# Graph attention: partial sums of k and v kept in one PSUM bank, and queries of two tiles by seven half-width products

## The chip, the cores and the metric

The kernel runs on one core of a Trainium2 chip. The metric is the device time of one execution in microseconds (us), lower is better, as the median of several runs. TensorE (PE in the profile) multiplies matrices into PSUM, which has eight banks of 128 partitions by 512 f32 values; VectorE (DVE) and ScalarE (ACT) read PSUM and do the elementwise work; GpSimd (POOL) issues the gathers; SyncE (SP) issues plain transfers.

## The reference

There are 16 graphs of 1024 nodes and 512 features, 8 heads of 64, and an adjacency matrix shared by all, in which nodes of low number have many neighbours and most have few. All inputs are f32.

```python
q = (x @ Wq + bq).reshape(b, n, H, HD)
k = (x @ Wk + bk).reshape(b, n, H, HD)
v = (x @ Wv + bv).reshape(b, n, H, HD)
scores = jnp.einsum('bqhd,bkhd->bhqk', q, k) / jnp.sqrt(jnp.float32(HD))
scores = scores + (1.0 - adj)[None, None, :, :] * -1000000000.0
attn = jax.nn.softmax(scores, axis=-1)
out = jnp.einsum('bhqk,bkhd->bqhd', attn, v).reshape(b, n, d) @ Wo + bo
...
x = _layernorm(x + out, axis=-1)
```

## The kernel before

The kernel finds the neighbours of each node at run time, sorts the nodes by their number of neighbours, and gathers `k` and `v` of a neighbour row by row, so that softmax runs only over edges. In each batch (a graph) the nodes lie in eight tiles of 128. One **block** is one neighbour of each of the 128 nodes of a tile; there are 530 blocks, 32 to 34 a batch.

**The work on a block** is spread over the steps of one large loop (its counter is `n`; it starts at -39 and ends after the last block). `gather` starts the transfer of the `k` and `v` rows into a tile `kvg`; `products` multiplies `k` by the query on VectorE (`qk`), `scores` sums by head (`s`), `exponentials` runs on ScalarE, and `weigh` multiplies `v` by the weights, either on ScalarE in eight activations of 64 columns or on VectorE in one instruction: `by_act` chooses. `add_own` adds up on VectorE; blocks of the few nodes with many neighbours go through a product on TensorE (`add_up`, bank `sum`). `normalise` divides, `turn` transposes the result (`poT`), and `finish` and `complete` multiply by `Wo` (`po`, through `product`) and do the residual and the layer norm.

**The fronts** make `q`, `k` and `v` of coming batches. `transpose_x` transposes a tile of `x` (`pxT`), `combine` makes four sums of halves of two tiles (`s1` to `s4`, each 128x256) and `pair(b, j)` lists the products of tiles 2j and 2j+1 as units. A query tile takes four products of 128x512 columns (`product`, line 799) and one VectorE instruction (line 830). `k` and `v` of the two tiles together take seven products of two halves each (`unit`, line 956), in the manner of Strassen and Winograd: the weights are combined once into `T1` to `T4`, and the products are added up in five banks: `x` (twice), `z` (twice), `p6`, `p7` and `p4`. ScalarE copies the first sum to `e` and the first `k` from bank `x` (lines 969, 835), and VectorE makes `w`, `g`, the second `k` and both `v` (lines 972, 975, 979, 984, 988). `squares` gives norms that a later test uses.

**The order** is written out by hand while the program is built. Each step places a fixed set of instructions and then takes units from a list (`finishing` before `fronts`) as long as its allowance of TensorE time (`credit`, fed by `share`) lasts; the costs of units are the constants `PRODUCT`, `SUM`, `TRANSPOSE` and `BIAS` in microseconds. A unit has a `ready` condition; if the first unit in the list is not ready, the step takes none. `later(k, fn)` puts an instruction k steps on, `later_last` at the end of such a step. Each engine then runs its instructions in that order, and waits for what it needs. PSUM is divided into four banks for `fill` (`pxT`, `poT`, `pq`, `po`, `p6`, `p7`, `p4` and small ones), two for `sum`, one for `x`, one for `z`. When the fronts have ended, tiles put aside in DRAM (`SPILL`) are finished, with the output bias added by a bf16 product (`bo_3` in three pieces, line 1090).

Of the kernel before, what the change touches and what calls it, by code (L numbers as in the profile page):

```python
# [10 lines left out]
F32 = mybir.dt.float32  # L11
# [39 lines left out]
ROWS = 3  # L51
# [18 lines left out]
LEAD_SHARE = 3.3  # L70
START_SHARE = 2.0
LAST_SHARE = 3.4
BIAS = 0.22

# [104 lines left out]
def kernel(  # L179
# [75 lines left out]
    with ExitStack() as main:  # L255
# [6 lines left out]
        def fill_psum(name):  # L262
            return psum.tile([P, HALF], F32, tag="fill", name=name, bufs=4)
# [19 lines left out]
        bo_3 = one.tile([P, D], BF16, name="bo_3")  # L283
        three = one.tile([P, 1], BF16, name="three")
# [4 lines left out]
        B12 = [None]  # L289

# [66 lines left out]
        def loads():  # L357
# [3 lines left out]
            nc.vector.tensor_scalar(bq_bc, bq_bc, scale, None, op0=OP.mult)  # L361
# [27 lines left out]
            yield  # L389
            broadcast(bo_bc, bo)  # L390
# [25 lines left out]
        def bias_norms():  # L416
# [10 lines left out]
            nc.vector.tensor_tensor(bk_bc, bq_bc, bq_bc, op=OP.mult)  # L427
            nc.vector.tensor_reduce(n8, bk_bc.rearrange("p (h d) -> p h d", d=HD), axis=AX.X, op=OP.add)
            nc.vector.tensor_reduce(bq_norm, n8, axis=AX.X, op=OP.max)

        def bias_pieces():

            r = work.tile([P, D], F32, tag="y", name="bo_rest", bufs=Y_BUFS)
            nc.vector.tensor_copy(bo_3, bo_bc)
            nc.vector.tensor_tensor(r, bo_bc, bo_3, op=OP.subtract)
            yield
            nc.vector.tensor_copy(bo_3[32:33, :], r[32:33, :])
            nc.vector.tensor_copy(bo_3[64:65, :], r[64:65, :])
            nc.vector.tensor_tensor(r[64:65, :], r[64:65, :], bo_3[64:65, :], op=OP.subtract)
            nc.vector.tensor_copy(bo_3[64:65, :], r[64:65, :])  # L440
            yield
            st = small.tile([P, 1], F32, name="two", bufs=1)
            nc.vector.tensor_tensor(st, ident[:, 0:1], ident[:, 32:33], op=OP.add)
            nc.vector.tensor_tensor(three, st, ident[:, 64:65], op=OP.add)

# [15 lines left out]
        def ranks():  # L461
# [55 lines left out]
            nc.vector.tensor_scalar(lone, ranked[:, 0, 1:2], 0.0, None, op0=OP.is_le)  # L517
# [24 lines left out]
        def more_ranks():  # L542
# [44 lines left out]
            for h in range(HEADS):  # L587
                sq = work.tile([P, D], F32, tag="ysq", name=f"sq_wq_{h}", bufs=1)[:, 0:NPAIR * HD].rearrange("p (c d) -> p c d", c=NPAIR)
# [48 lines left out]
        def edges(t):  # L637
# [63 lines left out]
            for i0 in range(0, nb, step):  # L701
# [8 lines left out]
                m = work.tile([P, D], F32, tag="qk", name=f"em_{t}_{i0}", bufs=2)[:, 0:n * J].rearrange("p (n j) -> p n j", n=n)  # L710
# [26 lines left out]
        BOTH = {}  # L737
        X, XT, SX, KV, VSUM, NRM, Y, OT, PS = {}, {}, {}, {}, {}, {}, {}, {}, {}
# [13 lines left out]
        def transpose_x(b, t):  # L752
            def pe():
# [5 lines left out]
                def out():  # L759
# [3 lines left out]
                    if t == 0 and b >= PAIRED_FROM:  # L763
# [6 lines left out]
                        sq = work.tile([P, D], F32, tag="ysq", name=f"sq_x_{b}", bufs=1)  # L770
# [9 lines left out]
                def combine():  # L780
                    s = [work.tile([P, HD2], F32, tag=f"s{i}", name=f"s{i}_{b}_{t}", bufs=1 + i // 4) for i in (1, 2, 3, 4)]
# [9 lines left out]
            return [(TRANSPOSE, pe, lambda: (b, t) in X)]  # L791

        def product(name, lhs, w, out):

            def unit(c):
                if c == 0:
                    PS[name] = fill_psum(name)
# [6 lines left out]
            return [(PRODUCT, lambda c=c: unit(c), None) for c in range(NPAIR)]  # L804
# [11 lines left out]
        def pair(b, j):  # L816
# [8 lines left out]
            def out_q(i, p):  # L825

                assert gathered[0] >= start[max(0, b - ROWS + 1)]
                tag, bufs = ("q", 2) if b or j else ("y", Y_BUFS)
                q = work.tile([P, D], F32, tag=tag, name=f"q_{b}_{tt[i]}", bufs=bufs)
                nc.vector.scalar_tensor_tensor(q, p, scale, bq_bc, op0=OP.mult, op1=OP.add)  # L830
# [34 lines left out]
            def mean_pe():  # L865
# [3 lines left out]
                def out():  # L869
                    m = work.tile([1, D], F32, tag="q", name=f"mean_{b}", bufs=2)  # L870
# [8 lines left out]
            def lone_product():  # L879
# [24 lines left out]

                return [(4 * BIAS, pe, None)]

            def lhs(i):
                return lambda c: XT[b, tt[i]][:, ts(c, P)]

            q0, q1 = (  # L910
                product(f"pq_{b}_{tt[i]}", lhs(i), W["q"], lambda p, i=i: out_q(i, p)) if b == 0 or tt[i] != ONE_KEY else []
                for i in range(2)
            )
            if j == 0 and b >= PAIRED_FROM:
                q0 = []
                if merged(b):
                    q0 = product(f"pq_{b}_0", lambda c: BOTH[b // 2][:, 1, c, :], W["q"], lambda p: out_q(0, p))
                    q0 += lone_product()
# [29 lines left out]
            def unit(bank, left, right, first, after, need):  # L948
                def pe():
                    if first:  # L950
                        R[bank] = fill_psum(f"p{bank}_{b}_{j}") if bank[0] == "p" else psum.tile(
                            [P, HALF], F32, tag=bank, name=f"{bank}_{b}_{j}", bufs=1
                        )
                    l = left()
                    for c in range(2):
# [6 lines left out]
                return [(2 * PRODUCT, pe, lambda: (need is None or need in R) and (b, j) in SX and bool(combined))]  # L962

            def temp(name):
                R[name] = work.tile([P, D], F32, tag=name, name=f"{name}_{b}_{j}", bufs=1)
                return R[name]

            def out_e():
                nc.scalar.copy(temp("e"), R["x"])  # L969

            def out_w():
                nc.vector.tensor_tensor(temp("w"), R["p6"], R["e"], op=OP.add)

            def out_g():
                nc.vector.tensor_tensor(temp("g"), R["p7"], R["w"], op=OP.add)

            def out_k1():
                kv = KV[b, tt[1]]
                nc.vector.tensor_tensor(kv[:, 0:D], R["p4"], R["g"], op=OP.add)  # L979
                send(1)  # L980
                later_last(1, lambda: norm(b, tt[1], kv[:, 0:D]))

            def out_v1():
# [674 lines left out]
```

## Time and profile before

| | us |
|---|---|
| median of 3 runs | 1856.82 |
| lowest, highest | 1855.36, 1866.84 |
| span of the profiled execution, first to last instruction | 1840.4 |
| PE, DVE, ACT, POOL busy in it | 1798.2, 1693.7, 1563.2, 1215.3 |

The runs are timed from outside the program, and the profile's span runs from the first to the last instruction of the program; the profiled execution's own time is given by its span alone. In the profile's rows a line such as L956 is a line of the kernel; out<-in names tiles without their numbers; after a count come the busy time in us, the mean length of one instruction in ns, and the idle time of the engine just before, with what ended it. Each f32 product appears as two matmul instructions. Their lengths overlap, since matmuls are pipelined and their ends are modelled. PEld is the loading of weights, and beside a stretch the granted clock of TensorE and the share of the DMA engines are given.

### The profile page before, as it was taken

Reading aid. Unit: us, or ns where it says so; the run is one execution under the profiler, and the core shown is the slowest. Engines: PE = TensorE matmul, PEld = TensorE weight load, DVE = VectorE, ACT = ScalarE, POOL = GpSimd, SP = SyncE. Lnnn points to the kernel's source line nnn. Section 1 sums busy time; section 2 is a strip of 40 time slices with the busy share of each in tenths; the row PEclk is TensorE's granted clock in tenths of the full one; section 3 lists DMA queues with packets and bytes.
Section 4 is the critical chain, followed back from the end, with each engine's and each line's share of the span. In section 5 each row is a group of like instructions: output and inputs, shape, how many; then the busy total and the mean of one; then the engine's idle time right before and its main releaser. Section 6 shows DMA issues by size and latency. Waiting matters only on the chain.

```text
span 1840.4 us, 25352 instructions
## 1 busy us (share of the span) xinstructions
PE 1798.2 (98%) x5140; PEld 876.2 (48%) x5140; DVE 1693.7 (92%) x3473; ACT 1563.2 (85%) x6183; POOL 1215.3 (66%) x1142
## 2 busy tenths in 40 slices
PE   7999999999999999999999999999999999999997
PEld 3444454554444454444444445444544444444443
DVE  6889889999989999999999999999999999997986
ACT  3637869989889898999889988989799999987886
POOL 1367766766565776767757666677666767665786
PEclk9999999999999999999999999999999999999998
DMA  7358787989889899999988998999989999889995
GB/s 287 106 190 253 256 325 237 346 301 327 308 280 314 295 336 319 344 316 308 347 316 310 346 335 276 343 321 322 339 315 325 314 355 326 306 324 325 338 319 191
DMA packets 198791, 558.54 MB, mean 303 GB/s; under 512 B 33450, under 2 KB 33470, under 8 KB 198626
## 3 DMA queue, kind: packets, MB, share of 16 engines
q0 software_dynamic: 112640, 370.50, 59.3%
q1 hardware_dynamic: 82910, 180.52, 26.2%
q10 hardware_dynamic: 3076, 5.82, 0.9%
q14 instruction: 122, 1.00, 0.2%
q8 instruction: 43, 0.70, 0.2%
HBM read 420.30 MB, written 157.45 MB: 314 GB/s over the span
## 4 chain that ended last, share of the span: by engine, by line
PE 69%; DVE 10%; ACT 9%; DMA 4%; issue 3%; POOL 1%; SPq 0%; POOLq 0%; DVEq 0%; ACTq 0%
PE po L799 17%; PE pq L799 15%; PE pp L956 12%; PE z L956 9%; PE x L956 9%; ACT pv L1341 5%; DVE qk L1313 2%; PE poT L1401 2%; PE pxT L757 2%; PE sum L1367 2%; DVE s L1317 2%; PE sum L1366 2%; DVE pv L1357 1%; ACT sq_k L809 1%; DMA kvg<-kv_pair,place_row 1%
## 5 line engine op out<-in xcount | busy, mean ns | idle before, releaser
L1341 ACT ACTIVATE pv<-kvg,pv 128x64 f32<-128x64 f32 x3600 | 907.5, 341 | 0.0
L1292 POOL DMA_INDIRECT kvg<-kv_pair,place_row x462 | 526.7, 1140 | 307.4 <-ACT pv L1341 99.6
L799 PE MATMUL pq<-wq,xT 128*128 128x512 f32 x792 | 367.8, 596 | 0.0
L1317 DVE TENSOR_REDUCE s<-qk 128x8 f32<-128x512 f32 x530 | 360.7, 681 | 6.8
L799 PE MATMUL po<-wo,oT 128*128 128x512 f32 x792 | 359.3, 594 | 0.7 <-ACT oT L1405 0.7
L1313 DVE TENSOR_TENSOR qk<-qt,kvg 128x512 f32<-128x512 f32 x434 | 297.2, 685 | 1.1 <-DMA kvg<-kv_rows,key_row 0.6
L956 PE MATMUL x<-b,xT 128*128 128x512 f32 x504 | 237.3, 593 | 0.5 <-ACT e L969 0.4
L956 PE MATMUL pp<-t,s 128*128 128x512 f32 x504 | 237.0, 593 | 0.0
L1357 DVE TENSOR_TENSOR pv<-pv,pv 128x520 f32<-128x520 f32 x329 | 228.3, 694 | 4.3 <-ACT pv L1341 4.2
L799 PEld LDWEIGHTS po<-wo,oT 128*128 128x128 f32 x792 | 149.1, 191 | 170.0 <-issue 160.2
L799 PEld LDWEIGHTS pq<-wq,xT 128*128 128x128 f32 x792 | 148.4, 192 | 161.9 <-issue 149.9
L1010 POOL DMA_INDIRECT x<-in_x_dram,asked_row x120 | 133.0, 1108 | 77.8 <-issue 21.3
L1148 POOL DMA_INDIRECT out_dram<-y,asked_row x129 | 146.9, 1139 | 39.1 <-issue 21.2
L1328 ACT ACTIVATE pv<-s,absent 128x8 f32<-128x8 f32 x434 | 127.0, 294 | 44.0 <-DVE s L1317 40.8
L809 ACT ACTIVATE sq_k<-kv 128x128 bf16<-128x128 f32 x512 | 150.8, 301 | 6.4 <-DVE kv L979 3.4
L956 PEld LDWEIGHTS pp<-t,s 128*128 128x128 f32 x504 | 94.7, 191 | 108.1 <-issue 99.4
L956 PEld LDWEIGHTS x<-b,xT 128*128 128x128 f32 x504 | 94.2, 191 | 107.4 <-issue 99.0
L956 PE MATMUL z<-b,s 128*128 128x512 f32 x252 | 119.2, 596 | 7.0 <-DVE kv L984 7.0
L1246 POOL DMA_INDIRECT qg<-q_rows,query_row x96 | 104.4, 1088 | 28.4 <-issue 26.9
L956 PE MATMUL z<-t,s 128*128 128x512 f32 x252 | 118.6, 593 | 0.0
L956 PE MATMUL pp<-t,xT 128*128 128x512 f32 x252 | 118.5, 593 | 0.0
L1134 ACT ACTIVATE y<-y,stats 128x512 f32<-128x512 f32 (+1 forms) x128 | 102.7, 806 | 17.0 <-DVE stats L1129 17.0
(279 smaller groups left out, 2713.0 us busy)
## 6 DMA issues: line engine op xcount, KB each, us to landing
kv_pair<-kv SPq DMA_DIRECT2D x98, 512.0 KB
q_rows<-q SPq DMA_DIRECT2D x106, 256.0 KB
qt<-q_rows SPq DMA_DIRECT2D x98, 256.0 KB
residual<-x SPq DMA_DIRECT2D x83, 256.0 KB
y<-residual SPq DMA_DIRECT2D x83, 256.0 KB
kv_rows<-kv SPq DMA_DIRECT2D x15, 512.0 KB
kvg<-kv_pair,place_row POOLq DMA_INDIRECT x462, 6.9
kv_pair<-kv SPq DMA_DIRECT2D x28, 256.0 KB
```

Source lines behind the costliest of these rows:

```text
L799: nc.tensor.matmul(p, lhs(c), w[:, c, :], start=(c == 0), stop=(c == NPAIR - 1))
L809: nc.scalar.activation(sq, s[:, ts(h, P)], AF.Square, scale=scale, accum_out=sums[:, h:h + 1])
L956: nc.tensor.matmul(R[bank], l[:, ts(c, P)], right[:, c, :], start=(first and c == 0), stop=(c == 1), skip_group_check=True,)
L1010: nc.gpsimd.indirect_dma_start(out=y, out_offset=None, in_=x_rows, in_offset=bass.IndirectOffsetOnAxis(ap=asked_row[:, t:t + 1], axis=0), ...
L1148: nc.gpsimd.indirect_dma_start(out=out_rows[b, t], out_offset=bass.IndirectOffsetOnAxis(ap=rows, axis=0), in_=y, in_offset=None, element_o ...
L1246: nc.gpsimd.indirect_dma_start(out=q, out_offset=None, in_=q_rows[b % ROWS], in_offset=bass.IndirectOffsetOnAxis(ap=rows, axis=0))
L1292: nc.gpsimd.indirect_dma_start(out=KG[n], out_offset=None, in_=rows, in_offset=bass.IndirectOffsetOnAxis(ap=(place_row if b else key_row)[ ...
L1313: nc.vector.tensor_tensor(QK[n], q, KG[n][:, 0:D], op=OP.mult)
L1317: nc.vector.tensor_reduce(S[n], QK.pop(n).rearrange("p (h d) -> p h d", d=HD), axis=AX.X, op=OP.add)
L1328: nc.scalar.activation(PV[n][:, D:], S.pop(n), AF.Exp, bias=bias)
L1341: nc.scalar.activation(pv[:, ts(h, HD)], v[:, ds(D + h * HD, HD)], AF.Copy, scale=pv[:, D + h:D + h + 1])
L1357: nc.vector.tensor_tensor(PV[b, t], PV[b, t], pv, op=OP.add)
```

## The change

- `k` and `v`: bank `x` now takes four of the seven products one after the other, and ScalarE copies it at four points, straight into the `kv` tiles. VectorE adds bank `z` twice and one `fill` bank (`p2`) once to what was copied.
- Queries: for pairs with `seven` (j above 0, without pair 1 of batch 0), the queries of the two tiles come from seven products of 128x256 columns with combined weights `TQ`, in a new bank `xq` and one half `fill` bank, with the bias added as a bf16 product (`bq_3`). ScalarE copies bank `xq` at four points, VectorE adds three times. The scaling of queries moves to the exponential.
- PSUM: three `fill` banks, one `xq`. At the end `po` may use `x`, `z` and `xq`.
- Order: `next_unit` takes the first ready unit among the next 12, but never passes a transpose; `combine` waits until the sums `s1` to `s3` of the pair before have been used.
- `by_act` gives fewer blocks to ScalarE (`turn_of % 3` in place of `% 2`); `qk` is written over the gathered `k`; some scratch tiles are bf16; `share` before step 0 is smaller.

```diff
-LEAD_SHARE = 3.3
-START_SHARE = 2.0
+LEAD_SHARE = 3.15
+START_SHARE = 1.85
+LOOK = 12
...
-            return psum.tile([P, HALF], F32, tag="fill", name=name, bufs=4)
+            return psum.tile([P, HALF], F32, tag="fill", name=name, bufs=3)
...
+        def query_weights():
+            top, low = W["q"][:, 0:2, :], W["q"][:, 2:4, :]
+            nc.vector.tensor_tensor(TQ[0], top[:, :, HD2:], top[:, :, 0:HD2], op=OP.subtract)
+            nc.vector.tensor_tensor(TQ[1], low[:, :, HD2:], TQ[0], op=OP.subtract)
...
                 def combine():
+                    if busy["s"]:
+                        later(1, combine)
+                        return
+                    busy["s"] = 3 if t == 1 or (b, t) == (0, 3) else 6
...
+                    spare = name[:2] == "po" and not fronts and not any(busy[k] for k in ("x", "z", "xq"))
...
-                nc.vector.scalar_tensor_tensor(q, p, scale, bq_bc, op0=OP.mult, op1=OP.add)
+                nc.vector.tensor_tensor(q, p, bq_bc, op=OP.add)
...
+            seven = j > 0 and (b, j) != (0, 1)
...
-            def out_e():
-                nc.scalar.copy(temp("e"), R["x"])
-
-            def out_w():
-                nc.vector.tensor_tensor(temp("w"), R["p6"], R["e"], op=OP.add)
-
-            def out_g():
-                nc.vector.tensor_tensor(temp("g"), R["p7"], R["w"], op=OP.add)
...
+            def copied(name, i, v, bank="x"):
+                def fn():
+                    if (b, tt[i]) not in KV:
+                        new_kv(i)
+                    nc.scalar.copy(half_of(i, v), R[bank])
+                    R[name] = True
+                return fn
+
+            def added(i, v, bank):
+                nc.vector.tensor_tensor(half_of(i, v), R[bank], half_of(i, v), op=OP.add)
...
+            kv1 = unit("x", lambda: a(0, 0), B11, True, copied("e", 0, False), None)
+            kv2 = unit("p2", lambda: a(0, 1), B21, True, out_k0, "e")
+            kv3 = unit("z", s(4), B22, False, out_v0, "v1")
+            kv4 = unit("x", lambda: a(1, 1), T4, False, out_k1, "g")
+            kv5 = unit("z", s(1), T1, True, out_v1, None)
+            kv6 = unit("x", s(2), T2, False, copied("w", 0, True), "e")
+            kv7 = unit("x", s(3), T3, False, copied("g", 1, True), "w")
+            if j == 0:
+                return kv1 + kv5 + xt + kv6 + q0 + kv2 + kv7 + q1 + kv4 + kv3
+            if not seven:
+                return kv1 + q0[:3] + kv6 + q0[3:] + xt + kv5 + kv7 + q1 + kv4 + kv2 + kv3
...
+            def begin():
+                busy["xq"] = True
+                Q["bank"] = psum.tile([P, D], F32, tag="xq", name=f"xq_{b}_{j}", bufs=1)
+                nc.tensor.matmul(
+                    Q["bank"], three.to_broadcast([P, P]), bq_3, start=True, stop=False, skip_group_check=True
+                )
+                multiply(Q["bank"][:, right], SX[b, j][0], TQ[0])
+                multiply(Q["bank"][:, left], a(0, 0), top[:, :, left])
...
+            def out_third():
+                new_q(1)
+                query_copied("g", 1, right)
+                query_added(1, right, Q["bank"][:, right])
+                Q["second"] = True
...
+            qu1 = query_unit(2 * PRODUCT + BIAS, begin, out_first, None, True)
+            qu6 = query_unit(
+                PRODUCT, lambda: multiply(Q["bank"][:, left], SX[b, j][1], TQ[1]), lambda: query_copied("w", 0, right), "e"
+            )
+            qu7 = query_unit(PRODUCT, lambda: multiply(Q["bank"][:, left], SX[b, j][2], TQ[2]), out_third, "w")
+            qu2 = query_unit(PRODUCT, second_bank, out_second, "e")
+            qu4 = query_unit(2 * PRODUCT, last_two, out_last, "second")
+            return qu1 + kv1 + kv5 + qu6 + kv6 + xt + qu7 + qu2 + kv7 + kv2 + qu4 + kv4 + kv3
...
-            QK[n] = work.tile([P, D], F32, tag="qk", name=f"qk_{n}", bufs=2)
-            nc.vector.tensor_tensor(QK[n], q, KG[n][:, 0:D], op=OP.mult)
+            QK[n] = KG[n][:, 0:D]
+            nc.vector.tensor_tensor(QK[n], q, QK[n], op=OP.mult)
...
-            return n < total - NBT and (turn_of % 2 == 0 or n < NBT // 2)
+            return n < total - NBT and (turn_of % 3 == 0 or n < NBT // 2)
...
+        def next_unit(units):
+            for i, (cost, _, ready) in enumerate(units[:LOOK]):
+                if cost == TRANSPOSE and i:
+                    return None
+                if not ready or ready():
+                    return i
+            return None
```

192 lines of the change are left out of this document (137 added, 55 removed).

## Prediction

> **What bounds the kernel now.** I read the busy line first, then the order of TensorE's instructions in a stretch of the middle, then the stretches and the waits.
>
> ```profile
> PE 1798.2 (98%) x5140; PEld 876.2 (48%) x5140; DVE 1693.7 (92%) x3473; ACT 1563.2 (85%) x6183; POOL 1215.3 (66%) x1142
> ```
>
> Three engines are near the span of 1840.4 us, so the share alone doesn't name the bound. The timeline does (start, us, then the group; two instructions make one f32 product):
>
> ```profile
> 908.65 0.59 PE L1366 MATMUL sum<-pv,sums 128*128 128x256 f32 x2
> 909.08 0.61 PE L1367 MATMUL sum<-pv,sums 128*128 128x264 f32 x2
> 909.53 1.88 PE L956 MATMUL z<-b,s 128*128 128x512 f32 x4
> 911.24 0.60 PE L1401 MATMUL poT<-ident,o 128*128 128x128 f32 x4
> 911.68 1.88 PE L956 MATMUL x<-b,xT 128*128 128x512 f32 x4
> 913.40 1.88 PE L956 MATMUL pp<-t,s 128*128 128x512 f32 x4
> 915.12 3.60 PE L799 MATMUL po<-wo,oT 128*128 128x512 f32 x8
> 918.55 0.60 PE L1401 MATMUL poT<-ident,o 128*128 128x128 f32 x4
> 918.99 3.60 PE L799 MATMUL pq<-wq,xT 128*128 128x512 f32 x8
> ```
>
> The printed lengths overlap; the true price is the distance of the starts. Two products of 512 columns take 1.72 us (911.68 to 913.40), four take 3.43 (915.12 to 918.55): 0.858 us each. One of 256 columns takes 0.43 (908.65 to 909.08). Nothing lies between the groups: whatever is taken out of this row comes out of the time, so long as the other two engines can follow.
>
> ```profile
> core 0: us, PE busy (x) PEld busy (x) DVE busy (x) ACT busy (x) POOL busy (x), PEclk, DMA share, GB/s
> 900.00:1020.00 120.00, 119.64 (x353) 58.98 (x352) 114.93 (x227) 110.65 (x456) 76.48 (x72) 1.00 0.91 321
> 1140.00:1260.00 120.00, 120.00 (x346) 59.05 (x345) 115.19 (x226) 115.00 (x477) 80.90 (x74) 1.00 0.91 322
> 1500.00:1620.00 120.00, 115.44 (x338) 56.89 (x337) 117.83 (x231) 114.18 (x479) 81.57 (x74) 1.00 0.93 329
> 1680.00:1740.00 60.00, 58.95 (x166) 28.26 (x165) 52.35 (x128) 47.48 (x155) 44.18 (x42) 1.00 0.95 343
> ```
>
> TensorE is full in the middle and nearly so in the end stage, at a granted clock of 1.00, but VectorE (DVE) has 2 to 5 us of 120 left and ScalarE (ACT) 5 to 9. A gain on TensorE alone would be stopped by them after a few per cent; what the change does to them is therefore part of the sum. Where does TensorE still wait, and who waits for it?
>
> ```profile
> PE z L956 <- DVE kv L984: 7.0, 5, 3.0
> PE x L956 <- ACT e L969: 0.4, 1, 0.4
> ACT e L969 <- PE x L956: 83.4, 36, 8.5
> ACT kv L835 <- PE x L956: 43.8, 28, 5.1
> DVE g L975 <- PE pp L956: 13.5, 16, 2.7
> ```
>
> (us in total, times, longest.) The largest wait of TensorE that lies in the repeated work is 7.0 us, for VectorE to have read bank `z`. The other way ScalarE alone waits 127.2 us for bank `x`. So TensorE sets the pace and the readers mostly stand ready.
>
> **The change, part by part.** The condition `seven` holds for pairs 2 and 3 of batch 0 and for pairs 1 to 3 of the 15 others: 47 pairs (the headline says 46; one pair is worth 0.6 us).
>
> *Queries on TensorE.* Removed per pair: eight products of 512 columns, 8 x 0.858 = 6.86 us. Added: fourteen of 256 (seven, each over two halves of K), 14 x 0.43 = 6.02, and the bias in bf16, whose price is here:
>
> ```profile
> 1752.11 0.38 PE L1090 MATMUL po<-bo,three 128*128 128x512 bf16 x1
> 1752.33 1.88 PE L799 MATMUL po<-wo,oTs 128*128 128x512 f32 x4
> L1367 PEld LDWEIGHTS sum<-pv,sums 128*128 128x128 f32 x192 | 36.6, 191 | 4.9
> ```
>
> That is 0.22 us. Together 6.24, a saving of 0.62 to 0.64 a pair; 47 pairs: **-30 us**. The `k` and `v` products keep their number and size. Is half the columns half the time when each product brings its own weights? The last row says that the 264-column products load theirs (192 loads of 191 ns) and still start 0.43 us after the 256-column ones: the loads are hidden.
>
> The Trainium skill, "TensorE: Matmul & The Clock Gate", section "The mechanism", speaks against this: weight loads overlap running products only where their row groups differ. Here both use all 128 rows, and the spacing of 0.43 us shows them hidden, so the trace decides; by that rule and the page's 107 ns for a load, 611 further loads would be an estimated 65 us and the sum would end near 1895. I keep the case as a rival, priced from the row.
>
> *Who reads the sums.* The rows with the prices:
>
> ```profile
> L972 DVE TENSOR_TENSOR w<-pp,e 128x512 f32<-128x512 f32 x63 | 43.0, 683 | 3.1 <-PE pp L956 1.6 <-ACT e L969 1.4
> L830 DVE SCALAR_TENSOR_TENSOR q<-pq,bq_bc 128x512 f32<-128x512 f32 x106 | 72.3, 682 | 11.0 <-PE pq L799 11.0
> L783 DVE TENSOR_TENSOR s<-xT 128x256 f32<-128x256 f32 x63 | 26.5, 420 | 7.9 <-ACT xT L761 4.9 <-PE z L956 3.0
> L969 ACT COPY e<-x 128x512 f32<-128x512 f32 x63 | 36.5, 580 | 83.4 <-PE x L956 83.4
> L730 ACT COPY sums<-pof 128x128 f32<-128x128 f32 x2 | 0.5, 246 | 0.0
> L1341 ACT ACTIVATE pv<-kvg,pv 128x64 f32<-128x64 f32 x3600 | 907.5, 341 | 0.0
> L1345 DVE TENSOR_TENSOR pv<-kvg,pv 128x512 f32<-128x512 f32 x80 | 54.9, 686 | 0.0
> ```
>
> For `k` and `v`, VectorE does three additions a pair in place of five, ScalarE four copies in place of two: over 63 pairs -126 x 0.683 = -86 us on VectorE, +126 x 0.580 = +73 on ScalarE. For the queries VectorE loses 94 x 0.682 = 64 us and gets 141 additions of 256 columns at 0.42 (the nearest row, L783) = 59; ScalarE gets 188 copies of 256 columns, between 0.246 (128 columns) and 0.580 (512), by the line through both 0.36, so 67 (46 to 109 at the ends). `by_act` with 3 in place of 2 moves weighings the other way: counted over the 530 blocks it falls from 450 to 393, 57 blocks. ScalarE's 3600 activations are busy 907.5 us, 2.02 for a block: -115; VectorE +57 x 0.686 = +39. The set-up of `TQ` and `bq_3` I put at 6 us on VectorE. Net: **VectorE -46 us (1648), ScalarE +25 (1588, at the ends +4 to +67)**. Against a span some 27 us shorter both keep their share, 91 and 88%. The in-place `qk`, the `ysq` in bf16 and the factor moved into the exponential change no count and no shape in those rows; I price them at nothing. They lie on VectorE and ScalarE; a tenth more on the 530 products `qk`, at 0.068 us each, would be 36 us on VectorE, which is less than the 46 it loses.
>
> *Banks and round trips.* The new cost is order. Four sums in `x` and three steps in `xq` mean that TensorE may not add to the bank before ScalarE has copied it: three trips a pair in `x` and three in `xq`, 63 x 3 + 47 x 3 = 330, where 126 were. `z` keeps one, but with twelve units around it, so its 7.0 us should go. What a trip costs depends on the work put between:
>
> ```profile
> 1059.28 1.88 PE L956 MATMUL z<-t,s 128*128 128x512 f32 x4
> 1060.99 1.88 PE L956 MATMUL pp<-t,xT 128*128 128x512 f32 x4
> 1065.88 1.98 PE L956 MATMUL z<-b,s 128*128 128x512 f32 x4 [3.01 <-DVE kv L984]
> ```
>
> Here only 1.72 us lay between, and 3 us were lost. `x` had at least 1.72, mostly 5.15 (`p6` and a query of 3.43) and lost 0.4 us in 63 trips, 6 ns each; `z`, with this short form in the pairs without a query, 7.0/63 = 111 ns each. The new order puts two to three units, 2.6 to 4.3 us, between, plus what comes of `po`, `poT` and `sum`. The bounds for 330 trips are thus 2 us and 37 us. I take 30 ns, 10 us, nearer to `x`, because the reader is again ScalarE, which waited for the bank in 36 of 63 copies.
>
> The Trainium skill, "Perfetto Trace Analysis", section "Matmuls", advises to rotate groups through different PSUM banks, so that reading one overlaps the next products. The old five-bank order does that and the new one gives it up. The `x` and `z` rows agree only where little lies between the two uses; by the rule alone the upper end would hold and the gain would vanish.
>
> Three `fill` banks in place of four: before, 128 `pxT`, 122 `poT`, 122 `po`, 106 `pq`, 189 of `p6`, `p7`, `p4` and 23 others use four, 172 each. After, some 517 use three, again 172. I price it at nothing; the cover is that load, and at the end `po` also gets `x`, `z` and `xq`. The looking-ahead in `next_unit` can only fill holes. The lower shares before step 0 follow the cheaper units and move work, they don't remove it.
>
> New waits on VectorE: the sum for the second query follows ScalarE's copy of the same half, once a pair. Behind it stand the block's `qk` and `s`; a copy takes 0.36 us and is the second thing in ScalarE's step, so 47 x 0.36 = 17 us at worst, inside VectorE's 46. SP issues the same stores; a query row leaves later, in one piece, and its readers come a batch later. The DMA engines, at 0.91 to 0.95 in the stretches above, move the same bytes in 1.5% less time; the end stage, at 0.95, shows TensorE still at 58.95 of 60.
>
> **The sum.** Profiled execution: 1840.4 - 30 - 7 + 10 = 1813.4 us of span. Outside the span lie 1856.8 - 1840.4 = 16.4 us, as the median of the runs shown stands to it; **1830 us**, 1.5% faster. These runs spread from 1855.4 to 1866.8, so I call within 1%, 1838 to 1875, no change.
>
> **The rivals.**
> 1. *All the gain and more*: trips as cheap as in `x`, and VectorE's 46 us free the holes of stages such as 1500 to 1620 (4.6 us of TensorE idle in 120): 1857 - 30 - 7 - 10 = 1810. For it: the readers wait. Against: more order.
> 2. *ScalarE becomes the bound* in the odd batches: there only 2 to 4 blocks leave it (4 to 8 us) while 140 us / 16 = 9 come. It has 115.0 of 120 in 1140 to 1260; some 118 in a stretch that is to be 118 leaves no gain. Half the batches lose theirs: 1857 - 15 = 1842.
> 3. *The copies come late* (slower): a copy queued behind a weighing of 2.02 us and the squares of a key tile reaches the bank after TensorE wants it. From 37/330 = 0.11 us a trip it eats everything, and `z` stood at just that; at 0.17 us it costs 56: 1857 - 37 + 56 = 1876.
> 4. *Loads not hidden*: 13 more a pair, 611 x 0.191 = 117 us at worst, 1857 - 27 + 117 = 1947; half shown, 1888. Against it stands 0.43.
> 5. *The change doesn't do what it says*: pairs wait in the list for a bank, steps go by with no unit, and the work saved comes back as holes: 1857.
>
> **Chances.** Forecast, 1812 to 1838: 0.60. Rival 1: 0.08. Rival 2: 0.12. Rival 3: 0.12, half of it above 1875. Rival 4: 0.03. Rival 5: 0.05. Faster by over 1%: forecast and rival 1, 0.68; slower: half of rival 3, rival 4 and a little of 5, 0.11; the rest, 0.21, within. The range 1808 to 1862 leaves out the dear half of rival 3, rival 4 and the far end of rival 1.
>
> **What would show it.** Query products of 256 columns 0.43 us apart, 1316 instructions of them; VectorE near 1648 busy, ScalarE near 1588; the wait of `z` for VectorE gone; TensorE's waits for ScalarE's copies of `x` and `xq` together near 10 us (over 37: rival 3); gaps ahead of `pxT`, `poT` or `p2` would say that three `fill` banks are too few. ScalarE at 118 of 120 in odd batches is rival 2. I am wrong if TensorE shows holes that no row of before shows.

## The result and the profile after

The changed kernel takes 1982.51 us (median of 4 runs, 1974.78 to 1983.27); the kernel before took 1861.83 beside it. The ratio is 1.0637 [1.0591, 1.0683]: 6.4% slower, where 1.5% faster was forecast. Of the 141 us between the spans of the two profiles (1981.5 and 1840.4) some 20 are not the change's: side by side the difference is 1982.51 - 1861.83 = 121 us.

The head and the busy line of the profile after:

```profile
span 1981.5 us, 26302 instructions
PE 1825.6 (92%) x5750; PEld 995.8 (50%) x5750; DVE 1655.0 (84%) x3464; ACT 1577.5 (80%) x6041; POOL 1207.4 (61%) x1143
```

All engines lost share: TensorE from 98 to 92%, VectorE from 92 to 84, ScalarE from 85 to 80. None became the bound over the span. TensorE's idle time (span less busy) went from 1840.4 - 1798.2 = 42 us to 1981.5 - 1825.6 = 156, so 114 of the 141 us are holes that were not there. By the groups view, 86 us of idle time stand ahead of the products into `x`, `z` and `xq`, where 7.5 stood ahead of `x` and `z`; ahead of `pxT` and `poT` it is 32, where it was 15. TensorE's busy time grew by 27 us, although it got less work; the last section offers a reason.

The same three stretches of the middle as in the prediction, in the windows view of after:

```profile
core 0: us, PE busy (x) PEld busy (x) DVE busy (x) ACT busy (x) POOL busy (x), PEclk, DMA share, GB/s
900.00:1020.00 120.00, 113.60 (x373) 63.77 (x372) 103.01 (x206) 100.83 (x387) 74.65 (x68) 0.97 0.86 295
1140.00:1260.00 120.00, 115.83 (x378) 63.02 (x377) 108.39 (x214) 108.56 (x429) 73.37 (x70) 1.00 0.93 324
1500.00:1620.00 120.00, 110.25 (x356) 61.47 (x354) 105.99 (x217) 96.25 (x369) 77.78 (x73) 0.99 0.85 295
```

TensorE has 4 to 10 us of holes in 120, VectorE 12 to 17, ScalarE 11 to 24. Where all three idle more, they wait for each other. The loss isn't even: the 53rd block has its scores 38 us later than before, and each further 53 blocks take from 1 us (blocks 266 to 318) to 18 us (160 to 212) longer, although up to block 477 ScalarE copies `x` and `xq` about as often in each, 39 to 47 times. The waits view of after (engine, line, for whom; us in total, times, longest):

```profile
PE z L998 <- DVE kv L1029: 41.5, 22, 4.7
PE x L998 <- ACT kv L1023: 17.2, 14, 3.3
PE poT L1555 <- DVE o L1541: 14.1, 3, 7.0
...
DVE q L1109 <- ACT q L1105: 50.4, 22, 6.2
DVE pv L1511 <- ACT pv L1495: 39.1, 36, 2.8
DVE q L1109 <- ACT xT L785: 17.3, 6, 3.8
...
ACT kv L1023 <- PE x L998: 123.1, 78, 7.2
ACT q L1105 <- PE xq L1076: 68.8, 48, 6.7
```

Bank `z`, whose 7.0 us were to go, now costs 41.5. The new addition to the second query (L1109) holds VectorE for 50.4 + 17.3 us. The waits form a ring: TensorE waits for VectorE, VectorE for ScalarE, ScalarE for TensorE. One turn of it, in the timeline of after (start, length, in brackets the idle time before and its releaser; ScalarE, VectorE, TensorE in turn):

```profile
682.50 0.80 ACT L1288 ACTIVATE y<-y,stats 128x512 f32<-128x512 f32 x1
...
684.81 0.64 ACT L795 ACTIVATE sq_x<-x 64x512 bf16<-64x512 f32 x1
685.43 0.57 ACT L785 COPY xT<-pxT 128x512 f32<-128x512 f32 x1
685.90 0.38 ACT L1105 COPY q<-xq 128x256 f32<-128x256 f32 x1
...
689.08 0.58 ACT L1023 COPY kv<-x 128x512 f32<-128x512 f32 x1
...
686.31 0.42 DVE L1109 TENSOR_TENSOR q<-xq,q 128x256 f32<-128x256 f32 x1 [4.16 <-ACT q L1105]
692.65 0.69 DVE L1029 TENSOR_TENSOR kv<-pp,kv 128x512 f32<-128x512 f32 x1
696.02 0.68 DVE L1029 TENSOR_TENSOR kv<-z,kv 128x512 f32<-128x512 f32 x1
...
681.96 1.03 PE L1076 MATMUL xq<-tq,s 128*128 128x256 f32 x4
...
690.13 1.88 PE L998 MATMUL x<-t,xT 128*128 128x512 f32 x4
696.76 3.78 PE L998 MATMUL z<-b,s 128*128 128x512 f32 x4 [4.74 <-DVE kv L1029]
```

The products into `xq` began at 681.96 and were done about 683. From 682.50 ScalarE ran without a gap, and its copy of `xq` came at 685.90, behind seven other activations and copies. VectorE stood still for 4.16 us until then, with the blocks behind it. The third copy of `x`, which the first `v` needs, began at 689.08 and was done by 689.66; but VectorE, busy without a pause from 686.31 on, reached its read of `z` only at 696.02, and TensorE waited 4.74 us for that bank. So this wait for `z` is VectorE's own lateness, from its stand-still, and not the third copy's.

Of the 22 waits for `z` (41.5 us in all) 14 are for the first `v`. Each time the third copy had landed 3.0 to 7.9 us before VectorE read the bank, with VectorE busy for nearly all of that. The four longest (4.74, 4.54, 3.92 and 3.63 us) follow a stand-still of VectorE of 3.3 to 4.5 us for ScalarE's copy of `xq`, at most 14 us earlier. Where TensorE waited long for `x` after the start-up, 2.62 us at 206.39 and 2.95 at 832.51, ScalarE was running a weighing of 2.0 us and squares for norms, ahead of the copy.

### The profile page after: what moved, and what is told of

It is laid out like the page before. It is cut to its first block, busy times and chain, and to the rows that moved or that the text cites. A ratio compares the mean times of both kernels' runs of the same rounds, so it can differ in the third digit from the quotient of the medians.

```text
span 1981.5 us, 26302 instructions
## 1 busy us (share of the span) xinstructions
PE 1825.6 (92%) x5750; PEld 995.8 (50%) x5750; DVE 1655.0 (84%) x3464; ACT 1577.5 (80%) x6041; POOL 1207.4 (61%) x1143
## 5 line engine op out<-in xcount | busy, mean ns | idle before, releaser
L1495 ACT ACTIVATE pv<-kvg,pv 128x64 f32<-128x64 f32 x3144 | 793.6, 342 | 0.4 <-issue 0.4
L1471 DVE TENSOR_REDUCE s<-kvg 128x8 f32<-128x512 f32 x530 | 360.7, 681 | 6.3
L1467 DVE TENSOR_TENSOR kvg<-qt,kvg 128x512 f32<-128x512 f32 x434 | 296.8, 684 | 6.2 <-DMA kvg<-kv_pair,place_row 6.2
L1023 ACT COPY kv<-x 128x512 f32<-128x512 f32 x252 | 146.3, 580 | 160.7 <-PE x L998 123.1
L1511 DVE TENSOR_TENSOR pv<-pv,pv 128x520 f32<-128x520 f32 x329 | 228.4, 694 | 44.1 <-ACT pv L1495 39.1
L998 PE MATMUL x<-t,s 128*128 128x512 f32 x504 | 240.9, 601 | 10.3 <-ACT kv L1023 10.0
L1076 PE MATMUL xq<-tq,s 128*128 128x256 f32 x564 | 149.1, 388 | 4.9 <-ACT q L1105 3.4
L1105 ACT COPY q<-xq 128x256 f32<-128x256 f32 x188 | 69.2, 368 | 92.7 <-PE xq L1076 68.8
L998 PEld LDWEIGHTS x<-t,s 128*128 128x128 f32 x504 | 93.2, 191 | 86.3 <-issue 67.1
L998 PE MATMUL x<-t,xT 128*128 128x512 f32 x252 | 122.4, 609 | 12.6 <-ACT kv L1023 7.2
L1076 PEld LDWEIGHTS xq<-tq,s 128*128 128x128 f32 x564 | 105.4, 194 | 53.6 <-issue 35.1
L998 PE MATMUL x<-b,xT 128*128 128x512 f32 x252 | 120.8, 602 | 2.2 <-ACT pv L1482 2.2
```

The lines of the kernel that those rows point to most:

```text
L998: nc.tensor.matmul(R[bank], l[:, ts(c, P)], right[:, c, :], start=(first and c == 0), stop=(c == 1), skip_group_check=True,)
L1023: nc.scalar.copy(half_of(i, v), R[bank])
L1076: nc.tensor.matmul(out, l[:, ts(c, P)], w[:, c, :], start=False, stop=(c == 1), skip_group_check=True)
L1467: nc.vector.tensor_tensor(QK[n], q, QK[n], op=OP.mult)
L1471: nc.vector.tensor_reduce(S[n], QK.pop(n).rearrange("p (h d) -> p h d", d=HD), axis=AX.X, op=OP.add)
L1495: nc.scalar.activation(pv[:, ts(h, HD)], v[:, ds(D + h * HD, HD)], AF.Copy, scale=pv[:, D + h:D + h + 1])
```

## The experiments

Three theories were put up. **A**: VectorE waits directly for ScalarE's copy of the same half. **B**: round trips: TensorE may add to a bank only after ScalarE, in its queue, has copied it. **C**: three `fill` banks are too few. Each ratio below is to the kernel before on the same chip, with its 95% interval.

**e1: the third addition one step later.** All else as after.

```diff
                 query_copied("g", 1, right)
+                later(1, third_added)
+            def third_added():
                 query_added(1, right, Q["bank"][:, right])
                 Q["second"] = True
```

> The changed kernel, with VectorE's addition for the second query (the one that in the same step follows ScalarE's copy of the same half) put one step later. Theory A, that this direct wait of VectorE on ScalarE (65 us of VectorE's idle time in the changed kernel's trace) delays VectorE and through it bank z and TensorE: most of the 120 us comes back, 1880 to 1920. Theory B, that the four sums in bank x, each to be copied by ScalarE before TensorE goes on, cost the time: little changes, 1960 to 1985. Theory C, that three fill banks are too few: little changes, 1960 to 1985.

1.0671 [1.0653, 1.0689]: no gain. VectorE's wait for the copy fell from 50.4 to 23.8 us, and this is in e1's waits of TensorE:

```profile
PE xq L1076 <- DVE q L1109: 46.9, 26, 4.3
...
PE z L998 <- DVE kv L1029: 22.7, 17, 4.4
```

The wait moved: TensorE now waits 46.9 us for `xq`, since its next products into that bank still need the addition, now a step later. A alone falls: moving this wait gains nothing. The cleaner test of it is e13, which takes the addition off the bank.

**e2: only the `k`/`v` part**, queries by eight products.

```diff
-            seven = j > 0 and (b, j) != (0, 1)
+            seven = False
```

> Only the k and v part of the change: queries by four products of 512 columns as before, bank xq unused, three fill banks, looking ahead and the lighter by_act as in the changed kernel. TensorE has 30 us of work more than in the changed kernel. Theory A (the direct wait in the query part): about the kernel before, 1850 to 1880. Theory B (bank x): most of the loss stays, 1940 to 2010. Theory C (three banks): the loss stays, 1940 to 2010.

1.0424 [1.0407, 1.0442]. Two thirds of the loss is there without any query of seven products.

**e3: only the query part**; `k` and `v` in five banks as before.

```diff
-            return qu1 + kv1 + kv5 + qu6 + kv6 + xt + qu7 + qu2 + kv7 + kv2 + qu4 + kv4 + kv3
+            return qu1 + x1 + p6 + qu6 + x2 + p7 + xt + qu7 + z1 + qu2 + p4 + qu4 + z2
```

> Only the query part of the change: seven products of 256 columns and bank xq as in the changed kernel, but the sums for k and v made as before in the banks x, z, p6, p7, p4 (e, w and g held in the kv tiles), with three fill banks. Theory A (the direct wait): the loss stays, 1940 to 1990. Theory B (bank x): the loss goes and the 30 us show, 1830 to 1870. Theory C (three banks, now with more users): 1960 to 2020.

1.0406 [1.0389, 1.0423]. Either part alone costs some 4%, together 6.4%: something is common to both.

**e4: the kernel before with three `fill` banks.**

```diff
-            return psum.tile([P, HALF], F32, tag="fill", name=name, bufs=4)
+            return psum.tile([P, HALF], F32, tag="fill", name=name, bufs=3)
```

> The kernel before with three fill banks in place of four and nothing else. Theories A and B: 1862 to 1890, since only waits of pxT, poT, pq and po for a free bank can come. Theory C: 1930 or more.

1.0184 [1.0167, 1.0201], 32 us: C is real, and more than a quarter of the loss. The group of the transposes, e4's row and then that of before (idle time behind the second bar):

```profile
L757 PE MATMUL pxT<-ident,x 128*128 128x128 f32 x512 | 74.2, 279 | 15.8 <-DMA x<-in_x_dram 6.9 <-DVE g L975 4.1 <-ACT oT L1405 2.0
```

```profile
L757 PE MATMUL pxT<-ident,x 128*128 128x128 f32 x512 | 70.0, 276 | 9.2 <-DMA x<-in_x_dram 7.1 <-ACT sums L730 1.4 <-DMA x<-in_x_dram,asked_row 0.4
```

`pxT` waits for the readers of `p7` and `poT`, which share its banks. These two waits are 6 us; TensorE's idle time grew by 22 in all (1873.6 - 1809.2 = 64 us). The Trainium skill's advice to rotate through different banks ("Perfetto Trace Analysis", section "Matmuls") is on the side of this run.

**e5: the frame**: five banks, plain queries, four `fill` banks; the looking ahead, the waiting `combine`, `by_act`, the shares, `qk` in place and the bf16 scratch tiles of the change stay. The cut leaves out the sums of `k` and `v`, put back as in e3.

```diff
-            seven = j > 0 and (b, j) != (0, 1)
+            seven = False
...
-            return psum.tile([P, HALF], F32, tag="fill", name=name, bufs=3)
+            return psum.tile([P, HALF], F32, tag="fill", name=name, bufs=4)
```

> What is left of the change without its two parts: looking ahead, by_act with 3, smaller shares, qk over the gathered k, with sums for k and v in five banks, queries by four products of 512 columns and four fill banks. If the losses measured so far add up (three banks 1.8%, k and v 2.4%, queries 2.3% net), nothing is left for the frame: within 1% of the kernel before. If looking ahead or the moved weighings are at fault: 2 to 3% slower.

1.0237 [1.0186, 1.0288]. With the additions left on VectorE, `by_act` puts it at 1733.4 us busy, 40 more than before, so e10 repeats it with the old rule.

**e6: `k`/`v` part with four `fill` banks**, as e2 otherwise.

```diff
-            return psum.tile([P, HALF], F32, tag="fill", name=name, bufs=3)
+            return psum.tile([P, HALF], F32, tag="fill", name=name, bufs=4)
```

> The k and v part alone with four fill banks (bank xq left out). Theory of trips (each of the three times that TensorE may add to bank x only after ScalarE has copied it holds both engines to the same step): 2 to 2.5% slower than before. Theory that three fill banks explain the k and v part: within 0.5%.

1.0264 [1.0215, 1.0312]: against e2's 1.0424, the fourth bank is worth 1.6 points here too.

**e7: two trips in bank `x` in place of three**, as e6 otherwise; the second `k` is added by VectorE from a `fill` bank, as before.

```diff
-            kv4 = unit("x", lambda: a(1, 1), T4, False, out_k1, "g")
+            kv4 = unit("p4", lambda: a(1, 1), T4, True, out_k1, "g")
```

> The kernel e6_kv_four_banks with the fourth product of bank x put back into a fill bank, and the second k made by VectorE as before: two trips in bank x a pair in place of three. Theory of trips: about a third to a half of the loss of e6_kv_four_banks goes, 1 to 1.7% slower than before. If the number of trips doesn't matter: as e6_kv_four_banks.

1.0277 [1.0217, 1.0337], the same as e6. TensorE's waits in e6, then in e7:

```profile
PE x L998 <- ACT kv L1023: 22.0, 19, 3.2
PE z L998 <- DVE kv L1029: 19.7, 17, 2.4
```

```profile
PE z L998 <- DVE kv L1038: 12.4, 8, 2.8
PE z L998 <- DVE kv L1029: 11.6, 7, 2.7
PE x L998 <- ACT kv L1023: 11.4, 10, 3.0
```

Waits for `x` halve, those for `z` grow from 19.7 to 24.0. B predicted a gain for each trip less; that dose is not shown. The trip less was not alone: VectorE is busy 1699.1 us in e7 and 1663.8 in e6.

**e8 and e9: less work on ScalarE**, in the kernel after and in the one before. The norms of the keys, which a later test uses, are left out and set to zero.

```diff
-            squares(f"k_{b}_{t}", k, NRM[b][:, t, :])
+                nc.gpsimd.memset(NRM[b], 0.0)
```

> The changed kernel without the squares that give the norms of the keys (left out: 512 activations with their reads of the sum, about 150 us of ScalarE). If the trips are dear because ScalarE reaches the copy late, behind its other work: 40 us or more faster than the changed kernel. If they are dear because ScalarE stands at the copy and waits for TensorE: less than 15 us.

> The kernel before without the squares that give the norms of the keys (left out, about 150 us of ScalarE): the control of e8_light_act. If TensorE paces the kernel before, within 1% of it. If ScalarE does wherever it is busy, 2% faster, as the changed kernel became by the same cut.

e8: 1.0435 [1.0387, 1.0484], 2.0 points or 38 us better than after, just short of the 40 named for copies that come late. e9: 0.9990 [0.998, 1.0], nothing. The busy lines of e8 and of e9:

```profile
PE 1817.4 (93%) x5750; PEld 994.6 (51%) x5750; DVE 1653.5 (85%) x3464; ACT 1438.2 (74%) x5017; POOL 1215.8 (62%) x1159
```

```profile
PE 1799.7 (98%) x5127; PEld 875.7 (48%) x5140; DVE 1693.1 (92%) x3473; ACT 1424.0 (77%) x5159; POOL 1216.9 (66%) x1158
```

139 us off ScalarE are worth something only where its copies stand inside TensorE's sums. It was idle for 20% of the span of after, and yet its queue counts. Through which bank is not shown: TensorE's idle time falls by 23 us (to 1950.6 - 1817.4 = 133), but the waits above for `z` and `x` only to 39.1 and 14.8.

**e15 and e16: the same test on VectorE.** The sum of `v` over the nodes, which its mean needs, is left out in both kernels.

```diff
-                    for v in kv:
-                        nc.vector.tensor_tensor(VSUM[b], VSUM[b], v, op=OP.add)
+                    pass
```

> The changed kernel without the additions that gather the mean of v (left out: 96 additions of 512 columns after the first of each batch, about 58 us of VectorE). Theory that the three engines are held together, so that each one's work counts: 12 to 25 us faster than the changed kernel (a quarter to a half of the cut, as for ScalarE). If VectorE has room, as its 84% says: less than 5 us.

> The kernel before without the same 96 additions, the control of e15_light_dve. If TensorE paces the kernel before: within 0.5%. If VectorE does in the stages where it is at 117 of 120: 1% faster.

e15: 1.0633 [1.0594, 1.0672], nothing to within 0.6 points, though VectorE is the busier of the two:

```profile
PE 1825.1 (91%) x5729; PEld 997.6 (50%) x5750; DVE 1595.8 (80%) x3368; ACT 1578.4 (79%) x6041; POOL 1211.1 (61%) x1143
```

e16: 0.9961 [0.9940, 0.9982]. That the load of all three engines together sets the time, as I held by then, falls: 59 us off VectorE changed nothing in after and 0.4% in the kernel before.

**e10, e11, e12, e17: `by_act` as before**, in e5, e6, after and e3.

```diff
-            return n < total - NBT and (turn_of % 3 == 0 or n < NBT // 2)
+            return n < total - NBT and (turn_of % 2 == 0 or n < NBT // 2)
```

> The kernel e5_frame with by_act as before (turn_of % 2: 57 weighings back on ScalarE). Theory of the moved weighings (in e5_frame VectorE is busy 1733 us, 39 more than before): within 0.7% of the kernel before. Theory of the order (looking ahead, combine that waits, smaller shares): 2% slower or more.

> The kernel e6_kv_four_banks (k and v part, four fill banks) with by_act as before. Theory of trips through bank x: 2 to 3% slower than before, as e6_kv_four_banks. Theory of the moved weighings: within 0.7%.

> The changed kernel with by_act as before. Theory of the moved weighings: 4% slower than before in place of 6.4%. If the loss comes from the two parts and the banks: 6 to 7% slower, or more, since ScalarE gets 110 us back.

> The query part alone (k and v sums in five banks, three fill banks) with by_act as before. Frame 1.3% and third fill bank 1.6 to 1.8% are in it: if the trips through bank xq just eat the 30 us of TensorE's work, 3% slower than before; if they cost more than that, 4% or more, if less, 1.5 to 2.5%.

e10: 1.0131 [1.0114, 1.0148]; e11: 1.0361 [1.0343, 1.0379]; e12: 1.0689 [1.0671, 1.0707]; e17: 1.0515 [1.0479, 1.0552]. The new rule relieves ScalarE: it loses 1.1 points in e5 and gains 1.0 in e6, 1.1 in e3 and 0.5 in after (the last hardly clear of its interval). With the old rule e10 is the frame without moved weighings; its 1.3 lies between the two theories, and both have a part. e11's 3.6 is more than the 2 to 3 named for trips, and e12's 6.9 is what was named for the two parts and the banks. Differences of runs with one rule can be read as parts. e17, over the 4% that meant dearer trips, less e10 and less what a `fill` bank costs (1.6 to 1.8), leaves 2.0 to 2.2 points for the queries; e12 less e11, taken side by side, and less the same bank leaves 1.4 to 1.7.

**e13: the third sum of `xq` read by ScalarE alone**, both halves in one copy; VectorE adds from SBUF later, off the path of the bank.

```diff
-                query_copied("g", 1, right)
-                query_added(1, right, Q["bank"][:, right])
-                Q["second"] = True
+                nc.scalar.copy(Q[1], Q["bank"])
+                Q["g"] = Q["second"] = True
+                later(1, lambda: nc.vector.tensor_tensor(Q[1][:, right], Q[1][:, left], Q[1][:, right], op=OP.add))
```

> The changed kernel with the third sum of bank xq read by ScalarE alone: one copy of 512 columns takes both halves (12 us more of ScalarE in all), and VectorE adds them one step later from SBUF, so that TensorE's next products wait for ScalarE only. Theory of two readers (TensorE waits for VectorE, which waits for ScalarE): 30 us or more faster than the changed kernel, 4.8% slower than before or less. Theory that every step holds the three engines together: within 0.7% of the changed kernel.

1.0563 [1.0525, 1.0600], 0.7 points better, which by itself is at the edge of the intervals. On the same chip, e14 and e15, which are as slow as after, took 1989.72 and 1993.13 us, and e13 1975.21: 14 to 18 us less, and in the profiles TensorE is idle for 156.0 us in place of 169.3 and 171.1. So one hand-over between two engines less in a bank's turn helps a little, about half of what the theory of two readers asked. TensorE's wait for VectorE's read of `z` falls from 41.5 us to this:

```profile
PE z L998 <- DVE kv L1029: 23.5, 15, 3.4
```

**e14: the last product of `z` one step later**, so that TensorE asks for the bank when VectorE has read it.

```diff
-                R["v1"] = True
+                if b < 2:
+                    R["v1"] = True
+                else:
+                    later(1, lambda: R.update(v1=True))
```

> The changed kernel with the second product of bank z allowed one step later after VectorE's addition of the first v (from batch 2 on). In the changed kernel's trace TensorE waits 41.5 us for that addition, which itself waits for ScalarE's third copy. If that wait is a cost of its own: 20 to 40 us faster than the changed kernel. If it only shows where the engines meet: the same time within 10 us, with the wait moved to other places.

1.0625 [1.0589, 1.0660], as after. The wait for `z` falls to 25.8 us, and one for VectorE's additions from `xq` grows from 4.2 to 20.2. As in e1, a hole moved in the order is not a hole less.

**e18: ScalarE's copies of `x` and `xq` at the end of its step**, behind the weighing of a block, 2.03 us in the timeline of after. VectorE's additions of the third and last sum of `xq` stand in the same functions and move with them.

```diff
-                    later(1, after)
+                    (later_last if bank == "x" else later)(1, after)
...
-                    later(1, after)
+                    (later if after is out_second else later_last)(1, after)
```

> The changed kernel with the copies of banks x and xq at the end of ScalarE's step, behind its weighing (some 2 us), in place of ahead of it. If the cost is that ScalarE stands at the copy, waiting for TensorE, and its weighings come late: 20 us or more faster than the changed kernel. If the cost is that TensorE waits until ScalarE reaches the copy: 20 us or more slower.

1.1055 [1.1006, 1.1105]: 4.2 points, 78 us, more for the same instructions in another order. TensorE's waits in e18:

```profile
PE x L998 <- ACT kv L1023: 63.9, 39, 5.7
PE z L998 <- DVE kv L1029: 33.0, 16, 5.4
PE xq L1076 <- ACT q L1105: 14.6, 10, 3.7
```

The wait for `x` is 63.9 us where it was 17.2, and by the groups view TensorE's idle time ahead of `x` and `xq` together is 125 us where it was 42: the holes for these two banks are about the whole of the 78 us. The place of the copy in ScalarE's queue prices a trip, and this is the strongest support for B.

**What the runs add up to**, in points of the time before. The list telescopes from before to after by construction; what is measured is each difference, to about 0.3 points between runs taken side by side and 0.5 to 0.7 between others.

| part | from | points |
|---|---|---|
| frame: looking ahead, waiting `combine`, shares, scratch tiles, `qk` in place | e10 | +1.3 |
| `k` and `v`: three trips in `x`, and `z` | e11 - e10 | +2.3 |
| `by_act` with 3 | e6 - e11 | -1.0 |
| one `fill` bank less | e2 - e6 | +1.6 |
| queries of seven products | after - e2 | +2.1 |
| sum | | +6.4 |

The queries' 2.1 points (39 us) are net of 29 us of products saved (worked out below), so their trips, with all else that is new in their order, cost about 68 us, 3.7 points. The groups view shows where two of these parts lie. From e10 to e11 TensorE's idle time ahead of `x` grows from 0.1 to 36.1 us and ahead of `z` from 11.0 to 16.0, together 41 us, for 42 us of time. From e2 to after the idle time ahead of `x`, `z` and `xq` grows from 42 to 86 us. None of the runs beats the kernel before.

## Why the prediction was wrong, step by step

**TensorE's work: right.** 1316 instructions of 256-column query products stand in the trace as said, one group of them in the groups view of after:

```profile
L1076 PE MATMUL xq<-tq,s 128*128 128x256 f32 x564 | 149.1, 388 | 4.9 <-ACT q L1105 3.4 <-ACT pv L1482 1.6
...
L1109 DVE TENSOR_TENSOR q<-xq,q 128x256 f32<-128x256 f32 x94 | 39.4, 419 | 69.3 <-ACT q L1105 50.4 <-ACT xT L785 17.3 <-ACT ysq L1274 0.8
L1105 ACT COPY q<-xq 128x256 f32<-128x256 f32 x188 | 69.2, 368 | 92.7 <-PE xq L1076 68.8 <-issue 17.4 <-remote 5.0
```

Two products in four instructions start 0.86 us apart (688.41 and 689.27 in the timeline of after), 0.43 each, so rival 4 (loads not hidden) is out, and the Trainium skill's rule on row groups ("TensorE: Matmul & The Clock Gate", section "The mechanism") was rightly set aside. By the distances of starts at full clock, an f32 instruction of 512 columns costs 0.429 us, one of 256 columns 0.215 and a bf16 one 0.22; 752 fewer, 1316 more and 46 more of them save 322 - 283 - 10 = 29 us, for 30 said.

**VectorE and ScalarE: right.** 1655.0 and 1577.5 us, for 1648 and 1588. A copy of a half took 0.368 us for 0.36 said. Rival 2 (ScalarE becomes the bound) is out by its own test: 108.56 of 120 in 1140 to 1260, not 118.

**The trips: the step that failed.** I gave 330 trips 30 ns each, 10 us, and 37 at most, from two banks of the old kernel whose reader stood ready; the runs put them at about 111. Three things were wrong in it.
- *The reader.* "ScalarE waited for the bank in 36 of 63 copies" was read as cover. It still waits (123.1 and 68.8 us above), in the same profile in which TensorE waits for it. An engine that waits often can still be late at the moment that counts, since it runs its instructions in the order written: e8, e9 and e18 show that ScalarE's queue now costs time. By the table, the trips of `x` and `z` cost 2.3 points (43 us) and those of `xq` some 68 us, together 111 us for 330 trips, 0.34 us each. This is over ten times the value taken, three times the upper bound; it lumps in every hand-over of the new order, and it is a mean, since some stretches lost almost nothing.
- *Bank `z`.* I looked at the units between its two uses and not at what its reader needs. The first `v` from `z` is added to `g`, the third copy of `x`, and takes its place in VectorE's order behind that copy and behind the blocks. In the trace the third copy was there in time, and VectorE, late in its order, was not. Units on TensorE around the bank don't help against that. Said: 7.0 us gone; found: 41.5 us.
- *The added wait on VectorE.* 17 us at worst, inside its slack; found 50.4 + 17.3 us. The copy was not "the second thing in ScalarE's step": in the turn above seven instructions ran between the product and it. VectorE's load as a whole counts for nothing (e15), but a stand-still of it delays its read of `z`: e1 and e13, which shorten or remove it, take TensorE's wait for `z` to 22.7 and 23.5 us.

**Three `fill` banks at nothing: wrong.** 172 uses a bank before and after was true and beside the point: e4, with more uses for each of three banks, shows 1.8% and e6 against e2 1.6. The cover named was the number of uses; that the time for which each use holds its bank counts in its place is my reading and was not tested.

**The frame at nothing: wrong**, 1.3% (e10). "The looking-ahead can only fill holes" is refuted for looking ahead, the waiting `combine`, smaller shares, scratch and in-place `qk` together; which of them does it was not separated.

**Outside the span: misread.** I took 16.4 us for time outside the span. The runs after list both: 1983.27 us with a span of 1981.5, so 1.8 us. The rest is most likely a difference between chips: in the later runs the kernel before took from 1844.82 us (beside e2) to 1874.83 (beside e17).

**The rivals.** Rival 3, copies queued behind other work, had the first link. By the sign that I set for it (over 37 us of TensorE's waits for ScalarE's copies) it would have been missed: these are 17.2 + 3.4 = 20.6 us, and the greater part of the lateness came by way of VectorE, as the 41.5 us for `z`. Its price, at most 0.17 us a trip, gave 1876; at 0.34 us it gives 1857 - 29 + 111 = 1939, and the frame with `by_act` (+0.3 points) and the bank (+1.6), some 35 us, leads to 1974. This is the table over again and no check of it. I gave rival 3 0.12. The 29 us saved are in this sum: they were gained, and lost several times over.

**What stays open.** Why two trips cost as much as three (e7); why some stretches lost almost nothing; what in the frame costs 1.3%; and how the trips' cost divides between ScalarE's lateness and the two-engine hand-overs, since e13 took one of those away and gained 0.7 points.

## What to carry to other kernels

Saving products by adding up, copying and adding up again in one bank makes the other engine's queue a part of TensorE's chain: price each trip by how far the copy can stand behind other instructions in that queue, not by the reader's share of busy time or by how often it waits. Follow each read of a bank to the last thing it needs and to its place in its engine's order, and count a PSUM bank taken from a rotating set as a cost of its own (here 1.6 to 1.8%). To learn which engine's queue counts, take work off it in both kernels: 139 us off an engine at 80% gave 2 points, and 59 us off one at 84% gave none.

## What was not expected of the chip

After a wait of TensorE in the middle of the work, the granted clock fell for some microseconds. Three stretches of 7 us around the wait shown above, in the windows view of after (columns as before, PEclk third from the end):

```profile
688.00:695.00 7.00, 4.01 (x14) 2.26 (x12) 6.97 (x14) 5.17 (x21) 5.71 (x6) 1.00 0.77 256
695.00:702.00 7.00, 5.24 (x6) 2.19 (x7) 4.71 (x12) 0.91 (x7) 5.60 (x6) 0.52 0.77 237
702.00:709.00 7.00, 7.00 (x29) 4.13 (x27) 6.17 (x12) 5.88 (x24) 2.34 (x2) 1.00 1.03 385
```

At 0.52 the products of `z` from 696.76 took 3.78 us where the same group took 1.88 elsewhere, so a hole of 4.74 us cost nearly 2 us more behind it. The Trainium skill, "TensorE: Matmul & The Clock Gate", section "What's actually happening", has the mechanism: an idle window of some 3.4 us halves the clock until a busy one. The half clock agrees, with 0.52; but shorter waits were enough here. Two more groups in the timeline of after, behind waits of 2.95 and 2.25 us:

```profile
832.51 3.78 PE L998 MATMUL x<-t,xT 128*128 128x512 f32 x4 [2.95 <-ACT kv L1023]
...
1681.21 3.34 PE L998 MATMUL z<-b,s 128*128 128x512 f32 x4 [2.25 <-DVE kv L1029]
```

The granted clock was 0.50 from 832.20 to 835.60 and 0.63 from 1680.80 to 1684.20. Between 300 and 1960 us there are a dozen such stretches in after. Over the span the mean clock is 0.976 for after, 0.996 for before, 0.991 for e10, 0.992 for e2 and 0.969 for e18. The kernel before shows 0.985 to 0.997 from run to run and chip to chip, so not all of this is the change: beside e12, which has 0.983, the kernel before has 0.993 to 0.996. For after the clock is thus at most 0.02 x 1981.5 = 40 us of TensorE's time, which is how its busy time could grow by 27 us with 29 us less work. Part of each price in the table is then the clock's, and a hole can cost more than its length.
